# Two attention and expert layers on one core: a new order of steps from a finer event model, imposed on every engine, with a shared variance for two norms

## The chip, the core and the metric

The kernel runs on one core of a Trainium2 chip. A core has TensorE (PE, matrix products into the PSUM banks), VectorE (DVE), ScalarE (ACT), GpSimd (POOL) and SyncE (SP, which here only issues transfers). The metric is the device time of one execution in microseconds, lower is better. Before the change three runs gave 536.8, 538.77 and 545.6; the median is 538.77.

## The reference, cut to what matters

`x` is 4 sequences of 512 tokens with 128 features. Two layers, each of the form x = x + s·g:

```python
x = L0_attn_x
xn = _layernorm(x, axis=-1)
s = _L0_attn_ref(xn, ...)           # causal window of 64, 16 heads of 8, 4 value heads
g = _silu(_L0_ffn_ref(xn, ...))     # 2 * (one of 8 experts, 128 -> 512 -> 128, gelu)
x = x + s * g
xn = _layernorm(x, axis=-1)
s = _L1_attn_ref(xn, ...)           # norm, windowed attention, projection, norm, gelu feed-forward
g = _silu(_L1_ffn_ref(xn, ...))     # one of 8 experts, 128 -> 512 -> 128, relu
x = x + s * g
return x
```

Layer 0's attention first takes the mean over all keys of the sigmoid of each masked score, makes a weight per query of it, and only then the softmax of the weighted scores, so each score tile is made twice (a first pass for the sums, a second for the softmax). Its output is multiplied by `w_o`, and `b_o` is added. Layer 1's attention starts with a second layer norm of the already normed `xn`: two norms stand behind each other, with an affine step after the second that is folded into other data.

## The kernel before, in words

Tokens are cut into 16 tiles of 128 (4 batches b with 4 tiles t). Attention goes by tile. The experts go by block: `route` (L316) sorts the tokens by expert into 23 blocks of 128 rows per layer. It makes the rank of each token, a matrix `tok_blk` (L377), the comparison `in_place` (L385), a matmul `tokens`, and from these the indices `which` (L403, the expert of each block, which the weight loads read), `tokens_at` and `put_at` (L413). `moe_load` (L421) then loads a block's weights through SP (two of 256 KB and a few small ones) and gathers its rows by an indirect transfer from POOL (`xb`, L435). `moe_x` transposes the rows (copy to `xbT`, L448), `moe_h` makes `hb` with gelu (L503) or ReLU (L506) on ACT, `moe_y` adds the bias on DVE (`yb`, L473) and puts the rows back by an indirect transfer (`yt`, L474). `gates` (L481) reads a batch back and makes its gate on ACT and DVE (L490, L491).

The work is written as 30 generator threads (list at L1235). A thread yields what it needs next; `run` (L204) takes the step with the earliest modelled ready time, and among equals the one with the lower rank from the table. `spent` (L191) books the modelled cost of a step: TensorE time, and durations on DVE (D), ACT (A) and POOL (G). This fixes TensorE's order, for `mm` and `turn` (L81, L87) stamp each matmul. The order on DVE, ACT and POOL was left to the framework's scheduler, apart from a few `high_priority` and `keep_in_program_order` marks, and `nc.any` copies out of PSUM went to DVE or ACT as that scheduler chose.

The parts that the change touches:

- The row constants `rowb` (L127), `colb`, `wo0_sb` and `v1c` (L141) come through ACT's queue, the inputs and other weights through SP's.
- `layernorm` (L254) takes statistics on DVE (`bn_stats` L259, `bn_aggr` L260), adds eps (L236), takes the power on POOL (`rsqrt`, L237), and scales on DVE (L272) or, for layer 0, on ACT after an offset (L265, L267). Layer 0's norms run once per batch at the start; `prepare0` transposes them (copy to `xnT`, L536).
- `scores_q` (L757) is the first pass of layer 0. Each tile fills two pairs of PSUM banks; per pair ACT makes `th` (tanh, L786) and DVE reduces `mx` from the bank and `sm` from `th` (both L788).
- `outs0` (L902) transposes the attention output, divides (L910, L911), copies the transpose to `attT` (L920), multiplies by `w_o`, and adds row `o0` on DVE into `s` (L928). `combine0` (L933) computes x = acc·s + x on POOL (L938, L939).
- `prepare1` (L945) norms the new x (`xr`), sends it to memory for the experts, and makes the expert logits (`lg`, L518). `project1` (L970) norms `xr` again (`xh`) and projects it.
- In layer 1 the maxima of the scores are at L1055, the copies `shd` at L1063, the exponentials at L1098 (layer 0: L880), the copies `osb` at L1121 (layer 0: L898), the context copy at L1173. `feed1` (L1176) adds the projection's bias to the residual on POOL (L1189), norms (`hn`), and does the feed-forward.

One fragment that a sentence can't say, the order of the first pass's readers (from L784):

```python
for gg in range(2):
    th = att_p.tile([P, 2, J * QW], F32, tag="th", name=f"th_{b}_{t}_{gg}", bufs=2)
    nc.scalar.activation(th, ps[gg], AF.Tanh, scale=0.5 * SCALE)
    for dst, src, op in ((mx, ps[gg], ALU.max), (sm, th, ALU.add)):
        nc.vector.tensor_reduce(
```

Of the kernel before, what the change touches and what calls it, by code (L numbers as in the profile page):

```python
# [9 lines left out]
F32 = mybir.dt.float32  # L10
# [47 lines left out]
def two_layers(  # L58
# [68 lines left out]
    nc.scalar.dma_start(rowb, rows.partition_broadcast(P))  # L127
    colb = weight(cols, [P, NCOL], "colb", engine=nc.scalar)
    wo0_sb = weight(wo0, [P, D], "wo0_sb", engine=nc.scalar)
# [7 lines left out]
    for c in range(2):  # L137
        for a in range(2):
            r = slice(64 * c + 32 * a, 64 * c + 32 * a + 32)
            nc.sync.dma_start(wproj_sb[r], wproj_h[c, a])  # L140
            nc.scalar.dma_start(v1c[r], v1_h[c, a, :, :, None])  # L141
# [31 lines left out]
    now = {"T": 6.0, "S": 0.0, "-": 0.0}  # L173
    free = [0.0] * 4
    busy = {e: [] for e in "DAGQ"}
    at = {}

    def slot(e, t, n):
# [5 lines left out]
        while True:  # L184
            t = max(t, b[i - 1][1]) if i else t
            if i == len(b) or t + n <= b[i][0]:
                b.insert(i, (t, t + n))
                return t + n
            i += 1

    def spent(cost, steps=(), events=(), scores=0):  # L191
        now["T"] += 1.12 * cost
        t = max(now["T"], now["-"]) + 0.2
        for i, (e, n) in enumerate(steps):
            t = slot(e, t, n) + 0.1 if e else t + n
            if i + 1 == scores:
                now["S"] = max(now["S"], t)
            if cost and not scores and i == 0:

                free.append(t)  # L200
        for e in events:
            at[e] = t

    def run(threads):  # L204

        asked = [(g, ranks, next(g)) for g, *ranks in threads]
        while asked:
# [22 lines left out]
            asked[i : i + 1] = [(g, ranks, new)] if new else []  # L230

# [22 lines left out]
    def layernorm(src, name, dst, scalar=False):  # L254

        mv = small.tile([P, NT, 2], F32, tag="mv", name=f"mv_{name}")
        for t in range(NT):
            st = small.tile([P, 6], F32, tag="st", name=f"st_{name}_{t}")
            nc.vector.bn_stats(st, src[:, t, :])  # L259
            nc.vector.bn_aggr(mv[:, t, :], st)  # L260
        rs = small.tile([P, NT], F32, tag="rs", name=f"rs_{name}")
        rsqrt(rs, mv[:, :, 1], LN_EPS)
        if scalar:
            off = small.tile([P, NT], F32, tag="off", name=f"off_{name}")
            nc.vector.scalar_tensor_tensor(off, mv[:, :, 0], -1.0, rs, ALU.mult, ALU.mult)  # L265
            for t in range(NT):
                nc.scalar.activation(  # L267
                    dst[:, t, :], src[:, t, :], AF.Identity, bias=off[:, t : t + 1], scale=rs[:, t : t + 1]
                )
            return  # L270
        for t in range(NT):
            nc.vector.tensor_scalar(  # L272
                dst[:, t, :], src[:, t, :], mv[:, t, 0:1], rs[:, t : t + 1], ALU.subtract, ALU.mult
            )

# [40 lines left out]
    def route(mask, n):  # L316
# [7 lines left out]
        with tc.high_priority():  # L324
# [53 lines left out]
            spent(0.35, [("D", 6.5)], [("rows", n)])  # L378
        yield "M", [("rows", n)]
        with tc.high_priority():  # L380
            ps = bank(f"tokens_{n}")
            for q in range(2):
                in_place = att_p.tile([P, NTOK // 2, P], BF16, tag="th", name=f"in_place_{n}_{q}", bufs=2)
                i = q * NTOK // 2
                nc.vector.tensor_tensor(  # L385
                    in_place, placef[:, i : i + NTOK // 2, None].to_broadcast([P, NTOK // 2, P]),
                    place_at[:, None, :].to_broadcast([P, NTOK // 2, P]), ALU.is_equal,
                )
                for u in range(NTOK // 2):
                    mm(  # L390
                        ps[:, 0 : 3 * NBLK], in_place[:, u, :], tok_blk[:, i + u].rearrange("p a k -> p (a k)"),
                        start=(i + u == 0), stop=(i + u == NTOK - 1),
                    )

            past = of([1, NBLK, E], "past")
            nc.vector.tensor_tensor(
                past, ends[0:1, None, :].to_broadcast([1, NBLK, E]),
                block_at[0:1, :, None].to_broadcast([1, NBLK, E]), ALU.is_le,
            )
            ofx = of([1, NBLK], "ofx")  # L400
            nc.vector.tensor_reduce(ofx, past, AX.X, ALU.add)
            which = of([1, NBLK], "which", I32)
            nc.vector.tensor_single_scalar(which, ofx, float(E - 1), ALU.min)  # L403
            tokf = of([P, NBLK], "tokf")
            nc.vector.tensor_copy(tokf, ps[:, NBLK : 2 * NBLK])
# [905 lines left out]
```

## Time and profile before

| | |
|---|---|
| median of three runs | 538.77 us |
| the profiled execution, its time | 559.01 us |
| its span (first to last instruction) | 557.3 us |
| mean granted TensorE clock | 0.874 |
| PE busy (5512 matmuls) | 416.5 us, 75% |
| DVE busy (992) | 346.3 us, 62% |
| ACT busy (496) | 257.9 us, 46% |
| POOL busy (255) | 189.9 us, 34% |
| moved by transfers | 42.08 MB, mean 76 GB/s |

The profiled execution is one run under the profiler and is longer than the median; a sum made from its rows is a sum against 559.01. Busy time is an average over stages. The stages here are: the start with norms, projections and routing (0 to 100 us), layer 0's attention beside its experts (100 to 244), the passage from layer 0 to layer 1 (244 to 362), layer 1's attention beside its experts (362 to 530), and the last batch's tail. A wait is shown as the engine that waits, its line, and the instruction whose end released it.

### The profile page before, as it was taken

How to read it: one execution, taken by the hardware profiler on the slowest of the kernel's cores; microseconds unless marked ns; L12 is line 12 of the kernel's file. 1: busy time of each engine (PE TensorE's matmuls, PEld its weight loads, DVE VectorE, ACT ScalarE, POOL GpSimd, SP SyncE). 2: the span in 40 equal slices, each digit the busy share in tenths (PEclk: the TensorE clock that was granted, in tenths of full speed). 3: DMA queues.
4: the chain of work that ended last, by engine and by line, in shares of the span. 5: the costliest groups of instructions: out<-in, count | busy, mean ns of one | idle time of the engine just before them, and what ended most of it. 6: DMA issues, size and time to landing. Idle time of an engine off the chain costs nothing. (4 is left out here: it accounts for less than half of the span.)

```text
span 557.3 us, 14273 instructions
## 1 busy us (share of the span) xinstructions
PE 416.5 (75%) x5512; PEld 295.9 (53%) x5512; DVE 346.3 (62%) x992; ACT 257.9 (46%) x496; POOL 189.9 (34%) x255
## 2 busy tenths in 40 slices
PE   1455347978886796876668595789997989978956
PEld 0343124656563475542435363577776867767654
DVE  4359858345675676677746679276736663747383
ACT  2312134577576445555233232257672665435721
POOL 4820033333442343027332320465634422333210
PEclk9957557898999988989669968799998999979998
DMA  5300612344333333002100001534563222340121
GB/s 161 95 11 1 171 44 58 84 131 117 89 108 103 102 89 95 8 16 76 38 21 2 1 21 43 149 98 133 142 170 102 51 61 42 85 110 22 54 75 39
DMA packets 61732, 42.08 MB, mean 76 GB/s; under 512 B 11297, under 2 KB 54049, under 8 KB 61665
## 3 DMA queue, kind: packets, MB, share of 16 engines
q1 hardware_dynamic: 58144, 34.47, 22.6%
q0 software_dynamic: 2944, 6.04, 4.4%
q8 instruction: 44, 0.72, 0.5%
q10 hardware_dynamic: 576, 0.66, 0.4%
q14 instruction: 24, 0.19, 0.1%
HBM read 34.99 MB, written 6.16 MB: 74 GB/s over the span
## 5 line engine op out<-in xcount | busy, mean ns | idle before, releaser
L474 POOL DMA_INDIRECT yt<-yb,put_at x46 | 46.7, 1016 | 114.2 <-DVE yb L473 56.8
L435 POOL DMA_INDIRECT xb<-xd,tokens_at x46 | 46.3, 1007 | 104.3 <-PE xt L88 50.4
L83 PE MATMUL y<-wb,hb 128*128 128x128 f32 x368 | 56.3, 308 | 3.6 <-issue 3.6
L83 PEld LDWEIGHTS y<-wb,hb 128*128 128x128 f32 x368 | 51.9, 220 | 9.3 <-issue 6.7
L83 PE MATMUL h<-xbT,wb 128*128 128x128 f32 x368 | 51.5, 288 | 2.5 <-DVE xbT L448 1.2
L83 PEld LDWEIGHTS h<-xbT,wb 128*128 128x128 f32 x368 | 46.9, 201 | 9.3 <-issue 6.0
L83 PE MATMUL e<-q,kd 32*64 32x256 f32 (+1 forms) x864 | 45.8, 471 | 6.2 <-DVE mx L1055 5.8
L1055 DVE TENSOR_REDUCE mx<-s 128x16 f32<-128x1024 f32 x32 | 37.7, 1219 | 17.5 <-PE s L83 13.2
L786 ACT ACTIVATE th<-s 128x768 f32<-128x768 f32 x32 | 24.3, 810 | 44.7 <-PE s L83 25.4
L1098 ACT ACTIVATE pt<-e 128x1024 f32<-128x1024 f32 x32 | 31.0, 1021 | 29.6 <-PE e L83 27.7
L788 DVE TENSOR_REDUCE mx<-s 128x8 f32<-128x768 f32 x32 | 30.4, 951 | 21.9 <-ACT th L786 21.9
L880 ACT ACTIVATE pt<-e 128x1024 f32<-128x1024 f32 x32 | 31.0, 1021 | 24.6 <-PE e L83 24.5
L83 PE MATMUL ov<-pt,va 64*32 64x128 f32 (+1 forms) x896 | 36.8, 310 | 3.1 <-issue 1.5
L83 PE MATMUL s<-k,qd 32*32 32x384 f32 (+1 forms) x1024 | 37.6, 473 | 0.5 <-ACT pt L1098 0.5
L506 ACT ACTIVATE hb<-h,bb 128x128 f32<-128x128 f32 x92 | 25.9, 375 | 17.0 <-PE h L83 12.1
L788 DVE TENSOR_REDUCE sm<-th 128x8 f32<-128x768 f32 x32 | 30.1, 942 | 0.0
L1014 POOL TENSOR_TENSOR q<-qd,jmask 128x640 f32<-128x640 f32 x16 | 20.0, 1256 | 27.8 <-PE e L83 16.1
L83 PEld LDWEIGHTS e<-q,kd 32*64 32x64 f32 x864 | 19.7, 145 | 18.1 <-issue 12.6
L1121 ACT COPY osb<-ov 128x512 f32<-128x512 f32 x19 | 10.8, 587 | 37.5 <-issue 24.6
L83 PEld LDWEIGHTS <-diag 32*32 32x32 bf16 (+1 forms) x304 | 5.5, 90 | 42.1 <-issue 40.6
L503 ACT ACTIVATE hb<-h,bb 128x128 f32<-128x128 f32 x92 | 25.7, 382 | 1.8 <-PE h L83 1.7
L83 PEld LDWEIGHTS ov<-pt,va 64*32 64x32 f32 (+1 forms) x896 | 19.5, 112 | 12.0 <-issue 4.0
(271 smaller groups left out, 905.4 us busy)
## 6 DMA issues: line engine op xcount, KB each, us to landing
wb<-in_w SPq DMA_DIRECT2D x92, 256.0 KB
bb<-in_b SPq DMA_DIRECT2D x46, 64.0 KB
acc<-yt SPq DMA_DIRECT2D x8, 256.0 KB
x<-in_x SPq DMA_DIRECT2D x4, 256.0 KB
xd<-ln_a SPq DMA_DIRECT2D x4, 256.0 KB
xd<-xr SPq DMA_DIRECT2D x4, 256.0 KB
out<-acc SPq DMA_DIRECT2D x8, 128.0 KB
bb<-in_cols SPq DMA_DIRECT2D x46, 2.0 KB
```

The lines of the kernel that those rows point to most:

```text
L83: ins = nc.tensor.matmul(*args, **kw)
L435: nc.gpsimd.indirect_dma_start(out=xb, out_offset=None, in_=xd, in_offset=bass.IndirectOffsetOnAxis(ap=tokens_at[:, k : k + 1], axis=0),)
L474: nc.gpsimd.indirect_dma_start(out=yt, out_offset=bass.IndirectOffsetOnAxis(ap=routed[n][0][:, k : k + 1], axis=0), in_=y, in_offset=None,)
L503: nc.scalar.activation(dst, src, AF.Gelu, bias=bias)
L506: nc.scalar.activation(dst, src, AF.Relu, bias=bias)
L786: nc.scalar.activation(th, ps[gg], AF.Tanh, scale=0.5 * SCALE)
L788: nc.vector.tensor_reduce(dst[:, t, 8 * gg : 8 * gg + 8].rearrange("p (u j) -> p u j", u=2), src.rearrange("p u (j f) -> p u j f", j=J), A ...
L880: nc.scalar.activation(pt[:, 2 * gg : 2 * gg + 2], ps[gg], AF.Exp)
L1014: engine.tensor_tensor(dst, src[:, None, o : o + TW].to_broadcast([P, J, TW]), jmask[:, :, None].to_broadcast([P, J, TW]), ALU.mult,)
L1055: nc.vector.tensor_reduce(mx.rearrange("p a g j -> p g a j")[:, 2 * gg : 2 * gg + 2], ps[gg], AX.X, ALU.max, negate=True,)
L1098: nc.scalar.activation(pt[:, 2 * gg : 2 * gg + 2], ps[gg], AF.Exp, scale=SCALE)
L1121: nc.any.tensor_copy(osb[:, :, :, w].rearrange("p a j f -> p (a j) f"), ov[w].rearrange("p a c d f -> p (a c d) f"))
```

## The change

- The event model knows more: slots for DVE, ACT and POOL in single steps, the ACT function tables ("Ae" for exp, "Ag" for gelu, 1.3 us for a switch), new durations, new ranks for the 30 threads. `traced` collects the instructions that each step issued, `spent` notes each one's modelled start, and `settle` links the instructions of DVE, ACT and POOL in the order of these starts. So the model's order holds on all engines.
- `copied` and `sooner` choose DVE or ACT for the copies out of PSUM by the model; so do layer 1's ReLU and the four masked copies k4 of layer 0. Copies to `shd` are always on ACT.
- `layernorm_twice`: the second norm of layer 1 takes no statistics. The normed data have mean 0 and variance v/(v+eps), so both scales come from v, by one power of eight columns; `xh` is made on ACT from x itself.
- Layer 0's sums: row `o0` is added by a matmul of one row per 128 tokens into the same bank; acc·s and + x are on DVE, straight from the bank where the gate is there in time, otherwise from a copy.
- `scores_q`: both maxima stand ahead of both tanh.
- `route`: no longer at high priority; `in_place` uses the buffers of layer 0's `osb` instead of those of `th`, `which` is made after it.
- Layer 0's norms: batches 0 to 2 at once, batch 3 after the first transpose. Only the first part of `rowb` stays on ACT's queue; the rest, `colb`, `wo0_sb` and `v1c` go to SP's.
- In `feed1` the residual's two bias additions on POOL are moved: one ahead into `contexts1`, one to just after the norm.

By the built program, TensorE gets 16 matmuls more, DVE has 11 k4 copies of 16 and 28 of the 92 ReLU pieces, ACT has 26 table loads where it had 32, and POOL loses 12 larger operations. TensorE's order is nearly the old one; in the tail, batch 2's last feed-forward steps now stand ahead of batch 3's projection.

```diff
         load_x(b)
     wqkv0_sb = weight(wqkv0, [P, 296], "wqkv0_sb")
     rowb = wts.tile([P, NROW], F32, tag="rowb", name="rowb")
-    nc.scalar.dma_start(rowb, rows.partition_broadcast(P))
-    colb = weight(cols, [P, NCOL], "colb", engine=nc.scalar)
-    wo0_sb = weight(wo0, [P, D], "wo0_sb", engine=nc.scalar)
+    first = _ROWS["o0"].start
+    nc.scalar.dma_start(rowb[:, 0:first], rows[0:first].partition_broadcast(P))
+    nc.sync.dma_start(rowb[:, first:NROW], rows[first:NROW].partition_broadcast(P))
+    colb = weight(cols, [P, NCOL], "colb")
+    wo0_sb = weight(wo0, [P, D], "wo0_sb")
...
     def spent(cost, steps=(), events=(), scores=0):
         now["T"] += 1.12 * cost
         t = max(now["T"], now["-"]) + 0.2
...
         for i, (e, n) in enumerate(steps):
-            t = slot(e, t, n) + 0.1 if e else t + n
+            if e and len(e) > 1:
+                t = max(t, now["table"])
+                if table[0] != e:
+                    n, table[0] = n + 1.3, e
+            if e:
+                t = slot(e[0], t, n)
...
+                    steps_of[e[0]] += [(t - n, len(steps_of[e[0]]) + k, x) for k, x in enumerate(ins[: share if same > 1 else None])]
+                if len(e) > 1:
+                    now["table"] = t
+                t += 0.1
+            else:
+                t += n
             if i + 1 == scores:
                 now["S"] = max(now["S"], t)
             if cost and not scores and i == 0:
 
                 free.append(t)
+        assert not runs, (steps, [(e, len(r)) for e, r in runs])
         for e in events:
             at[e] = t
...
             at[e] = t
 
+    def sooner(cost, a, d, start=0.0):
+
+        t = max(now["T"] + 1.12 * cost, now["-"], start) + 0.2
+        ends = {}
+        for e, n in (("A", a), ("D", d)):
+            ends[e] = slot(e, t, n, take=False)
+        return min(ends, key=ends.get)
+
+    def copied(dst, src, cost, events=(), a=0.6, d=0.7):
+        e = sooner(cost, a, d)
+        (nc.scalar.copy if e == "A" else nc.vector.tensor_copy)(dst, src)
+        spent(cost, [(e, a if e == "A" else d)], events)
+
+    def settle():
+
+        for e, steps in steps_of.items():
+            steps.sort(key=lambda s: s[:2])
+            for (*_, one), (*_, next_) in zip(steps, steps[1:]):
+                tc.add_manual_dep(
+                    next_, one.name, mybir.DependencyInfo(mybir.DependencyClass.NoSync, mybir.DependencyReason.DATA),
+                    reason="order",
+                )
+
     def run(threads):
 
+        traced(skip=True)
...
+        settle()
 
...
+    def layernorm_twice(src, b, dst):
+
+
+        mv = moments(src, f"b{b}")
+        w = small.tile([P, 2, NT], F32, tag="w2", name=f"w2_{b}", bufs=1)
+        nc.vector.tensor_scalar_add(w[:, 0], mv[:, :, 1], LN_EPS)
+        nc.vector.reciprocal(w[:, 1], w[:, 0])
+        nc.vector.tensor_tensor(w[:, 1], w[:, 1], mv[:, :, 1], ALU.mult)
+        nc.vector.tensor_scalar_add(w[:, 1], w[:, 1], LN_EPS)
+        rs = small.tile([P, 2, NT], F32, tag="rs2", name=f"rs2_{b}", bufs=1)
+        nc.gpsimd.tensor_tensor(
+            rs.rearrange("p a t -> p (a t)"), w.rearrange("p a t -> p (a t)"),
+            neghalf[:, 0:1].to_broadcast([P, 2 * NT]), ALU.pow,
+        )
+        for t in range(NT):
+            nc.vector.tensor_scalar(
+                dst[:, t, :], src[:, t, :], mv[:, t, 0:1], rs[:, 0, t : t + 1], ALU.subtract, ALU.mult
+            )
+        both = small.tile([P, 2, NT], F32, tag="twice", name=f"twice_{b}", bufs=B)
+        nc.vector.tensor_tensor(both[:, 1], rs[:, 0], rs[:, 1], ALU.mult)
+        nc.vector.scalar_tensor_tensor(both[:, 0], mv[:, :, 0], -1.0, both[:, 1], ALU.mult, ALU.mult)
+        return both[:, 0], both[:, 1]
 
...
-            spent(0.35, [("D", 6.5)], [("rows", n)])
-        yield "M", [("rows", n)]
-        with tc.high_priority():
-            ps = bank(f"tokens_{n}")
-            for q in range(2):
-                in_place = att_p.tile([P, NTOK // 2, P], BF16, tag="th", name=f"in_place_{n}_{q}", bufs=2)
...
+            spent(0.35, [("D", 1.0)] * 7, [("rows", n)])
+        in_places = []
+        for q in range(2):
+            in_place = att_p.tile([P, NTOK // 2, P], BF16, tag="osb0", name=f"in_place_{n}_{q}")
+            i = q * NTOK // 2
...
+                in_place, placef[:, i : i + NTOK // 2, None].to_broadcast([P, NTOK // 2, P]),
+                place_at[:, None, :].to_broadcast([P, NTOK // 2, P]), ALU.is_equal,
+            )
+            in_places.append(in_place)
...
+        which = of([1, NBLK], "which", I32)
+        nc.vector.tensor_single_scalar(which, ofx, float(E - 1), ALU.min)
+        spent(0, [after(("rows", n))] + [("D", 0.75)] * 4, [("places", n)])
+        yield "M", [("places", n)]
+        ps = bank(f"tokens_{n}")
+        for i in range(NTOK):
...
-            spent(0.13, [("A", 0.3)], [("mx", n, k)])
+            copied(x_k, ps[:, 0:P], 0.13, [("mx", n, k)], 0.28, 0.28)
 
...
+        return "Ag", 1.5
+
+    def relu(h, src, bias):
+        e = sooner(0.92, 1.5, 1.4)
+        for c in range(FC):
+            dst, src_c, b = h[:, c, :], src[:, c * P : (c + 1) * P], bias[:, c : c + 1]
+            if e == "A":
+                nc.scalar.activation(dst, src_c, AF.Relu, bias=b)
+            else:
+                nc.vector.tensor_scalar(dst, src_c, b, 0.0, ALU.add, ALU.max)
+        return e, 1.5 if e == "A" else 1.4
...
+    def norm0(b):
+        xns[b] = tok.tile([P, NT, D], F32, tag="ln", name=f"ln_a{b}", bufs=3)
         layernorm(x_sb[b], f"a{b}", xns[b], scalar=True)
         put_tokens(xd0, b, xns[b])
-        spent(0, [("D", 2.2), ("G", 1.0), ("D", 0.2), ("A", 1.5)], [("ln0", b)])
+        spent(0, [(None, 1.5 * b), ("D", 1.5), ("G", 1.0), ("D", 0.2), ("A", 1.7)], [("ln0", b)])
...
+    traced(skip=True)
+    with tc.high_priority():
+        for b in range(3):
+            norm0(b)
...
+            if b == 0:
+                norm0(3)
             yield "M", [("xnT0", b)]
...
                     )
+            def over_keys(dst, src, gg, op):
+                nc.vector.tensor_reduce(
+                    dst[:, t, 8 * gg : 8 * gg + 8].rearrange("p (u j) -> p u j", u=2),
+                    src.rearrange("p u (j f) -> p u j f", j=J), AX.X, op,
+                )
+
+            for gg in range(2):
+                over_keys(mx, ps[gg], gg, ALU.max)
+            spent(1.5, [("D", 1.9)], scores=1)
             for gg in range(2):
                 th = att_p.tile([P, 2, J * QW], F32, tag="th", name=f"th_{b}_{t}_{gg}", bufs=2)
                 nc.scalar.activation(th, ps[gg], AF.Tanh, scale=0.5 * SCALE)
-                for dst, src, op in ((mx, ps[gg], ALU.max), (sm, th, ALU.add)):
-                    nc.vector.tensor_reduce(
-                        dst[:, t, 8 * gg : 8 * gg + 8].rearrange("p (u j) -> p u j", u=2),
-                        src.rearrange("p u (j f) -> p u j f", j=J), AX.X, op,
-                    )
-            spent(1.3, [("D", 1.9)], scores=1)
-            spent(0, [("A", 1.65), ("D", 1.9)], [("s0", i)], scores=1)
+                over_keys(sm, th, gg, ALU.add)
+                spent(0, [("A", 0.83), ("D", 0.95)], [("s0", i)], scores=1)
 
     def fitness0():
 
         for b in range(B):
-            yield "M", [("s0", b * NT + NT - 1), ("ke", (b - 1) * NT - 1)]
+            yield "-", [("s0", b * NT + NT - 1)]
             mx, sm = mxs[b]
             qk = qks[b]
 
...
-            yield "M", [("attT", b), ("xnT0", B - 1)]
+            copied(attT, transposed(att0[b], f"att_{b}"), 0.5, [("attT", b)])
+            yield "M", [("attT", b)] + ([("x1", b - 1)] if b - 1 in s0 else [])
             ps = bank(f"s0_{b}")
             for u in range(NT):
-                mm(ps[:, u * D : (u + 1) * D], attT[:, u * P : (u + 1) * P], wo0_sb, start=True, stop=True)
-            s = tok.tile([P, NT, D], F32, tag="xt", name=f"s0_{b}", bufs=B)
-            s0[b] = s
-            nc.vector.tensor_tensor(
-                s, ps.rearrange("p (t d) -> p t d", t=NT), row("o0")[:, None, :].to_broadcast([P, NT, D]), ALU.add
-            )
-            spent(1.1, [("D", 0.7)], [("so", b)])
+                o = ps[:, u * D : (u + 1) * D]
+                mm(o, ones[0:1, :], row("o0")[0:1], start=True, stop=False)
+                mm(o, attT[:, u * P : (u + 1) * P], wo0_sb, start=False, stop=True)
+            ps = ps.rearrange("p (t d) -> p t d", t=NT)
+            if at.get(("gate", 0, b), 1e9) < now["T"] + 3.0:
+                combine(b, ps)
+                spent(1.5, [("D", 0.7), ("D", 0.7)], [("so", b), ("x1", b), ("acc", 0, b)])
+            else:
+                s0[b] = tok.tile([P, NT, D], F32, tag="s0", name=f"s0_{b}", bufs=1)
+                copied(s0[b], ps, 1.5, [("so", b)])
+
+    def combine(b, s):
+
+        acc = accs.pop((0, b))
+        nc.vector.tensor_tensor(acc, acc, s, ALU.mult)
+        nc.vector.tensor_tensor(x_sb[b], acc, x_sb[b], ALU.add)
 
...
             yield "-", [("x1", b)]
             xn = tok.tile([P, NT, D], F32, tag="xt", name=f"xr_{b}", bufs=B)
             xrs[b] = xn
-            layernorm(x_sb[b], f"b{b}", xn)
+            twice[b] = layernorm_twice(x_sb[b], b, xn)
             put_tokens(xd1, b, xn)
...
         for b in range(B):
             yield "-", [("xn1", b), ("s1", (b - 1) * NT - 1)]
-            xh = tok.tile([P, NT, D], F32, tag="ln", name=f"xh_{b}", bufs=B)
-            layernorm(xrs[b], f"c{b}", xh)
-            at["xh", b] = slot("D", slot("G", slot("D", at["xn1", b], 2.3), 1.0) + 0.2, 1.4)
+            xh = tok.tile([P, NT, D], F32, tag="ln", name=f"xh_{b}", bufs=3)
+            scaled(xh, x_sb[b], *twice[b])
+            spent(0, [("A", 1.7)], [("xh", b)])
...
-            nc.any.tensor_copy(shd, transposed16(shb.rearrange("p a g r -> p a (g r)"), 2, f"sh1_{b}_{t}"))
+            nc.scalar.copy(shd, transposed16(shb.rearrange("p a g r -> p a (g r)"), 2, f"sh1_{b}_{t}"))
             sh4 = att_p.tile([P, 2, J, P], BF16, tag="sh4_1", name=f"sh4_1_{b}_{t}")
             for j in range(J):
...
+                nc.gpsimd.tensor_tensor(xrs[b], xrs[b], projb[:, None, :].to_broadcast([P, NT, D]), ALU.add)
+                spent(0, [("G", 1.6)], [("res", b)])
...
-            nc.gpsimd.tensor_tensor(res, res, projb[:, None, :].to_broadcast([P, NT, D]), ALU.add)
             nc.vector.tensor_tensor(res, ps.rearrange("p (t d) -> p t d", t=NT), res, ALU.add)
-            hn = tok.tile([P, NT, D], F32, tag="ln", name=f"hn_{b}", bufs=B)
+            hn = tok.tile([P, NT, D], F32, tag="ln", name=f"hn_{b}", bufs=3)
             layernorm(res, f"d{b}", hn)
-            spent(1.9, [("D", 0.7), ("D", 2.3), ("G", 1.0), ("D", 1.4)], [("pr", b)])
...
+            nc.gpsimd.tensor_tensor(res, res, row("ffn2")[:, None, :].to_broadcast([P, NT, D]), ALU.add)
+            spent(0, [after(("pr", b)), ("G", 1.3)])
             yield "M", [("pr", b)]
             hT = tok.tile([P, T], F32, tag="hT", name=f"hT_{b}", bufs=1)
```

## The prediction

> **What bounds the kernel now.** I read the share of busy time first (TensorE 75%, DVE 62%, ACT 46%, POOL 34%), cut the span into stages by what the work is, then read TensorE's waits, and then the timeline at each long one. The stages (columns: window, length, busy time of PE, its weight loads, DVE, ACT, POOL, then granted clock, DMA share, GB/s):
>
> ```profile
> 0.00:100.00 100.00, 47.62 (x367) 31.31 (x368) 63.40 (x210) 28.94 (x52) 34.25 (x94) 0.70 0.27 75
> 100.00:244.00 144.00, 116.67 (x1422) 79.73 (x1420) 89.38 (x198) 87.32 (x160) 46.75 (x51) 0.94 0.34 90
> 244.00:362.00 118.00, 82.89 (x1176) 52.49 (x1183) 77.34 (x245) 37.83 (x60) 39.85 (x38) 0.81 0.16 43
> 362.00:530.00 168.00, 152.32 (x2473) 119.94 (x2458) 100.67 (x297) 97.56 (x217) 66.37 (x71) 0.97 0.34 89
> 530.00:557.30 27.30, 17.03 (x96) 12.39 (x94) 15.51 (x43) 6.21 (x11) 2.68 (x2) 0.87 0.20 58
> ```
>
> TensorE idles 52.4, 27.3, 35.1, 15.7 and 10.3 us in these five, 140.8 in all. No engine is full in the first or third stage, so those are chains of dependent steps; in the fourth TensorE is busy 91%, so little can be taken there. Who ends TensorE's waits (total, times, longest):
>
> ```profile
> PE s L83 <- DVE mx L788: 22.6, 13, 7.9
> PE tr_xn L88 <- ACT ln_a L267: 12.4, 1, 12.4
> PE e L83 <- DVE mx L788: 8.7, 7, 2.4
> PE s L83 <- DVE attT L920: 7.6, 1, 7.6
> PE tokens L83 <- DVE in_place L385: 6.3, 2, 4.9
> PE e L83 <- DVE mx L1055: 6.1, 2, 5.8
> ...
> PE tr_o L88 <- DVE lg L518: 4.5, 1, 4.5
> PE tokens L83 <- DVE tok_blk L377: 4.3, 1, 4.3
> ```
>
> Two things stand out. Layer 0's score tiles wait for the maxima that DVE takes from their banks (L788), and the long single waits of the third stage are on DVE. The DVE timeline before TensorE's 7.6 us wait:
>
> ```profile
> 267.28 1.11 DVE L272 TENSOR_SCALAR xh<-xr,mv_c,rs_c 128x128 f32<-128x128 f32 x4 [0.71 <-POOL rs_c L237]
> 268.31 0.48 DVE L259 BATCH_NORM_STATS2 st_b<-x 128x6 f32<-128x128 f32 x2
> 268.71 0.16 DVE L260 BATCH_NORM_AGGREGATE mv_b<-st_b 128x2 f32<-128x6 f32 x1
> 268.79 0.66 DVE L920 COPY attT<-tr_att 128x512 f32<-128x512 f32 x1
> ```
>
> One 0.66 us copy that TensorE needs stands behind the chained norm (xh) of another batch and even behind statistics that nothing needs yet: a wrong order, not a shortage of DVE.
>
> **What the Trainium skill says.** "PSUM — Partial Sum Buffer", section "PSUM bank collisions raise a hardware error": two engines may not be in one bank and quadrant at once, two readers included. So th (ACT) and mx (DVE) of one bank must take turns; the trace agrees, DVE mx waits 21.9 us in 14 places for ACT th. "ScalarE: Activation LUTs", section "What ACT_TABLE_LOAD costs": 1283 ns for the load, 2.66 us with the drain; the trace shows 32 loads of 1283 ns, and the drain is no row in it. "TensorE: Matmul & The Clock Gate", Part 1: idling drops the clock to half and sustained activity restores it; here eight h matmuls take 0.89 us at full clock and 2.08 at half, and about 141 us of the execution are at half clock. The same page, under "Architectural detail", calls ACT's and DVE's queues strictly first in, first out; the copy above agrees.
>
> **The change part by part.** Sums are on the profiled execution (559.01 us, of which 557.3 are the span and 1.7 lie around it). The median of the three runs, 538.77, is 0.9638 of it; I scale by that at the end.
>
> *mx before th (L786, L788).* Before, a tile reads th0, mx0, sm0, (th1 beside sm0), mx1, sm1. With th 0.81, mx 0.95, sm 0.94, the second bank comes free 0.81+0.95+0.94+0.95 = 3.65 us after its scores. After, mx0, mx1, th1: 0.95+0.95+0.81 = 2.71, so 0.94 earlier. The second stage holds 14.2 us of these waits in 14 places (s 9.3, e 4.9); 14 × 0.94 = 13.2 is the most. Some will be ended by another thing, such as ACT's own queue: I take −10 (−4 to −16; a table load less there is in the lower end).
>
> *The order pinned on DVE, ACT and POOL.* By itself it does no work. It pays where a late DVE step holds TensorE: in the third stage attT 7.6, mx of layer 1 6.1, lg 4.5, tok_blk 4.3, osb of layer 1 3.4, together 25.9. Not all can vanish, for batch 3's x must be finished, normed and routed before the experts of layer 1 can start. The next two edits shorten that chain. I take −18 (−8 to −24) for all three.
>
> *Chained norm from the first variance.* Per batch it removes 4 st_c (0.275), 4 aggregates (0.171) and a pow from the chain, and adds about seven small DVE operations at the 0.17 of the L236 row: 1.8 against 1.2 us. The scaling, 4 × 0.44, goes from DVE to ACT (4 × 0.48 by the L267 row). From x to xh I count 10.5 us before and 7.5 after. DVE loses 16 × 0.446 + 16 × 0.441 − 4.8 = 9.4 us, ACT gains 7.7; ACT has 80 us free in that stage. Counted in the −18. If ACT were full there, it would cost its 1.9 us per batch.
>
> *Layer 0 sums from the bank.* Removed: four 0.69 us adds on DVE (L928) and 1.28 + 1.38 on POOL per batch (L938, L939). Added: two DVE operations of about 0.69 (row L491: 0.68) and 16 one-row matmuls. No row shows a one-row matmul; the nearest are 128-column ones at 0.11 (full clock) and 0.29 (mean of h). 16 × 0.11 to 16 × 0.29 is 1.8 to 4.6, and none hidden, since TensorE waits beside attT anyway: I take +2. The combine itself is 1.3 shorter per batch, also in the −18.
>
> *Fewer table loads.* The built program has 26 in place of 32, and in the part that matches the fourth stage 5 in place of 11. The loads there before:
>
> ```profile
> L503 ACT ACT_TABLE_LOAD x16 | 20.5, 1283 | 0.3
> L1098 ACT ACT_TABLE_LOAD x5 | 6.4, 1283 | 4.6 <-PE e L83 4.5
> ```
>
> 6 × 1.28 = 7.7 us of ACT (16 with the skill's drain). TensorE has only 15.7 us idle there; I take −4 (−8 to +6: a fixed order may put a late step ahead of a ready one in the densest stage).
>
> *Copies and ReLU by the model.* 7 blocks' ReLU go to DVE, all shd copies and 5 k4 masks to ACT: about 10 us each way. Nothing, while DVE is at 60% and ACT at 58% of the fourth stage; without that cover it is 1.5 us per block.
>
> *Start: layer norm 0, DMA queues, routing.* I walked the new order with the old durations. DVE now waits for POOL's pow before xnT_0 (POOL has masks to build), so xnT_0 comes at 19 instead of 15.7; q and k are normed at 37.6 instead of 42.1; the expert mask at 47.4 instead of 43.5; the last routing row (put_at) at 69.3 either way. Moving colb, wo0 and v1c from ACT's queue to SP's, past the inputs and the rest of rowb, frees ACT's first norm of a wait for v1c (8.9 to 9.9), but the norm's off is late as well. 0 (−4 to +4).
>
> *Tail.* After batch 3's last context, the new TensorE order puts batch 2's last feed-forward steps before batch 3's projection. TensorE idles 10.3 there, so most is hidden: +1 (0 to +4).
>
> Sum: −10 −18 +2 −4 +0 +0 +1 = −29. 559.01 − 29 = 530.0, × 0.9638 = 511.
>
> **The rivals.**
> (A) The stalls only move. DVE's work and TensorE's order are nearly the same, and each named wait may be followed by the next step of the same chain. Then the third stage gives nothing: −10 −4 +2 +1 = −11, 548 × 0.9638 = 528. For it: POOL's pow and the routing chain remain. Against it: the rows above show unneeded work ahead of needed work.
> (B) More than forecast, since shorter idling keeps the clock up. All 25.9 gone, 14.2 of mx, 7.7 of table loads, and the third stage's clock from 0.81 to 0.94: 82.9 × (1 − 0.81/0.94) = 11.5. Less 3 added: −56, 503 × 0.9638 = 485. Against it: it needs each to come in full.
> (C) Slower. ACT's order is now fixed by a model. In the 16 layer 0 score tiles th can stand behind a gelu of an expert block or an exp whose own input is late; then both banks stay taken, and TensorE's next scores wait. To be over 2% slower (549.5, that is 570.2 profiled, +11.2) it has to eat the other 29 as well: 40.2 / 16 = 2.5 us per tile. ACT's th waited 14.1 us in 4 places for the h of an expert block before, up to 4.8 each, so 2.5 is possible in a tile, but in all 16 it needs a model that is wrong everywhere.
> (D) It does not do what it says: the fixed order equals the old in the stalls. The result is A's.
>
> **How the numbers follow.** Forecast 0.55 (its own range 497 to 525), A with D 0.20, B 0.14, C 0.11. About 2% is what a measurement of this kernel can tell from no change: 528 to 549.5. A straddles that edge: 0.09 faster, 0.11 the same; of C 0.03 is the same and 0.08 slower. Faster 0.55 + 0.14 + 0.09 = 0.78, same 0.14, slower 0.08. The range 484 to 537 takes in A with the bad ends of the start and the tail (+8 profiled) and B's figure; it leaves out about half of B and most of C.
>
> **What would show it.** Right: the waits of s and e for mx fall from 31.3 to under 15; those on attT, lg, tok_blk and layer 1's mx are gone or under 2 each; the third stage is 15 us or more shorter, and xh follows x by 7 to 8 us; 26 table loads; put_at still near 69. Wrong: ACT's th waiting behind hb or pt, a third stage of the same length with new names in TensorE's waits, a start that is over 4 us longer, or a fourth stage with TensorE under 88%.

## The result and the profile after

The changed kernel takes 542.71 us (median of 20 runs, 540.39 to 547.49), the kernel before 538.77 (20 runs, 532.79 to 547.9): a ratio of 1.0118, with an interval of 1.0086 to 1.0149. It is a little slower, where 511 and a range of 484 to 537 were forecast. The ratio compares fast executions alone, those up to 1.5% above the fastest of their kernel (all 20 after, 13 of 20 before), so it lies above the quotient of the two medians.

The stages of the profile after, cut at the same events as below (end of the first put_at, of the second, of the last put; columns: window, length, busy time of PE, its weight loads, DVE, ACT, POOL, then granted clock, DMA share, GB/s):

```profile
0.00:68.50 68.50, 27.46 (x164) 18.44 (x165) 42.79 (x169) 17.16 (x32) 22.63 (x80) 0.89 0.29 82
68.50:332.40 263.90, 221.49 (x2851) 143.21 (x2851) 180.29 (x447) 151.94 (x276) 81.49 (x88) 0.86 0.24 66
332.40:507.50 175.10, 150.40 (x2418) 121.08 (x2420) 108.21 (x300) 82.85 (x190) 71.92 (x74) 0.92 0.37 96
507.50:541.20 33.70, 22.63 (x131) 15.11 (x117) 17.04 (x45) 10.34 (x15) 2.53 (x3) 0.81 0.22 65
```

Against the first profile of before (put_at at 69.3 and 350.3, last put at 524.9) the middle is 17 us shorter and layer 1's attention with its experts the same. But that profiled execution, with its 559.0 us, is above all 20 plain runs of its kernel. A second profile of the kernel before (first experiment) is the fairer measure; there layer 1 takes 159.5 us, and after it takes 175.1. TensorE's waits after the change:

```profile
PE s L83 <- ACT th L925: 19.9, 14, 8.6
PE xt L88 <- DMA xb<-xd,tokens_at: 16.7, 8, 3.7
PE e L83 <- POOL q L977: 6.5, 3, 3.9
...
PE s L83 <- DVE attT L263: 1.1, 2, 0.8
...
PE e L83 <- DVE mx L1194: 1.0, 2, 0.5
```

The long waits on attT, on layer 1's maxima, lg and tok_blk are gone, as forecast. The maxima of layer 0 no longer end a wait of the scores; the tanh that now stands behind them does. New is the second line: a block's transposition waits for its gathered rows, which are POOL's work. The masked q of the third line is POOL's work too, and not new: the scores waited 0.4 us for it in the first profile of before and 3.3 in the second. POOL's waits before, and then after the change:

```profile
POOL yt L474 <- DVE yb L473: 56.8, 15, 11.1
POOL xb L435 <- PE xt L88: 50.4, 15, 11.3
```

```profile
POOL yt L579 <- DVE yb L577: 84.7, 21, 12.2
...
POOL yt L579 <- DMA yt<-yb,put_at: 29.3, 10, 4.2
```

POOL stands 114 us in front of puts (68.7 before: 56.8 and 11.9), for the block's result on DVE or for the landing of the put before. Nothing is seen to pass a waiting put in either kernel: both profiles of before start POOL's 255 instructions in one and the same order, both of the changed kernel their 243. What differs is where the gathers stand in that order. When a gather is issued (from the fifth of a layer on), the gathers ahead of it are four to seven more than the puts in the kernel before, and one to three more in the changed one. The POOL timeline of one such place, and TensorE's line for the block whose gather it holds up:

```profile
404.96 1.05 POOL L311 TENSOR_TENSOR rs_d<-rs_d,neghalf 128x4 f32<-128x4 f32 x1 [8.42 <-DVE rs_d L310]
406.21 1.14 POOL L579 DMA_INDIRECT yt<-yb,put_at  x1 [0.20 <-issue]
...
412.68 0.99 POOL L579 DMA_INDIRECT yt<-yb,put_at  x1 [3.92 <-DMA yt<-yb,put_at]
417.35 0.97 POOL L579 DMA_INDIRECT yt<-yb,put_at  x1 [3.67 <-PE f L83]
...
419.76 1.01 POOL L541 DMA_INDIRECT xb<-xd,tokens_at  x1 [0.16 <-issue]
```

```profile
424.19 0.45 PE L88 MATMUL xt<-ident,xb 128*128 128x128 f32 x1 [3.69 <-DMA xb<-xd,tokens_at]
```

The three puts had their rows from DVE by 405.7, so the second waits for the landing of the put before, as its line says, and the third most likely too (the profile names PE's f, which that put doesn't read). The gather at 419.76 is the first since 386.43. In the median, without the first four gathers of each layer, a gather before the change was issued 28 us (layer 0) and 21 us (layer 1) ahead of its transposition; after it, 4.4 and 8.4 us, and 19 of all 46 had under 5 us.

Why the gathers came to stand there can be read in `moe_load` (L529 of the changed kernel; the same in the old one). It books a block's weight loads and its gather as one step, which may start when y of the block four earlier is done, since the weights take over that block's buffers. The put of that earlier block is booked from the same moment on, so the order made from the bookings sets the gather behind it. The gather itself needs only the buffer `xb`, which is free once the earlier block is transposed: it was issued 0.7 and 1.5 us after that before the change (medians of the two layers), and 17 and 21 us after it in the changed kernel. A version that books the gather by `xb` alone was not run.

### The profile page after: what moved, and what is told of

Read it like the earlier page. It is cut to its first block, busy times and chain, and to the rows that moved or that the text cites. A ratio compares the mean times of both kernels' runs of the same rounds, so it can differ in the third digit from the quotient of the medians.

```text
span 541.2 us, 14293 instructions
## 1 busy us (share of the span) xinstructions
PE 422.0 (78%) x5544; PEld 297.8 (55%) x5544; DVE 348.3 (64%) x959; ACT 262.3 (48%) x512; POOL 178.6 (33%) x243
## 4 chain that ended last, share of the span: by engine, by line
PE 44%; DVE 21%; ACT 9%; DMA 9%; issue 8%; POOL 8%; SPq 0%; POOLq 0%; ACTq 0%; DVEq 0%
PE s L83 9%; PE e L83 7%; PE y L83 5%; PE h L83 5%; DMA xb<-xd,tokens_at 4%; DMA yt<-yb,put_at 4%; PE ov L83 3%; PE fy L83 3%; ACT th L925 3%; PE f L83 2%; DVE mx L915 2%; ACT pt L1014 2%; DVE mx L1194 2%; PE o L88 1%; DVE xr L372 1%
## 5 line engine op out<-in xcount | busy, mean ns | idle before, releaser
L83 PE MATMUL e<-q,kd 32*64 32x256 f32 (+1 forms) x864 | 47.3, 479 | 7.4 <-POOL q L977 6.5
L83 PE MATMUL y<-wb,hb 128*128 128x128 f32 x368 | 52.8, 295 | 0.1
L83 PEld LDWEIGHTS y<-wb,hb 128*128 128x128 f32 x368 | 48.7, 208 | 5.6 <-ACT hb L608 2.5
L925 ACT ACTIVATE th<-s 128x768 f32<-128x768 f32 x32 | 26.0, 812 | 45.7 <-DVE mx L915 44.9
L1014 ACT ACTIVATE pt<-e 128x1024 f32<-128x1024 f32 x32 | 31.0, 1021 | 20.3 <-PE e L83 20.2
L83 PE MATMUL s<-k,qd 32*32 32x384 f32 (+1 forms) x1024 | 39.1, 510 | 0.9 <-DVE k L1155 0.5
L83 PE MATMUL ov<-pt,va 64*32 64x128 f32 (+1 forms) x896 | 31.3, 302 | 4.6 <-DVE att L1290 4.4
L263 ACT COPY osb<-ov 128x512 f32<-128x512 f32 x36 | 20.1, 589 | 29.4 <-PE ov L83 26.1
L608 ACT ACTIVATE hb<-h,bb 128x128 f32<-128x128 f32 x92 | 25.9, 379 | 2.4 <-PE h L83 2.3
L88 PE MATMUL xt<-ident,xb 128*128 128x128 f32 x46 | 14.0, 316 | 16.7 <-DMA xb<-xd,tokens_at 16.7
L616 ACT ACTIVATE hb<-h,bb 128x128 f32<-128x128 f32 x64 | 18.2, 374 | 15.6 <-PE h L83 12.3
L83 PEld LDWEIGHTS ov<-pt,va 64*32 64x32 f32 (+1 forms) x896 | 18.1, 111 | 11.4 <-issue 5.9
```

Of the source, the lines that this page charges most:

```text
L83: ins = nc.tensor.matmul(*args, **kw)
L88: ins = nc.tensor.transpose(dst, src, ident)
L263: (nc.scalar.copy if e == "A" else nc.vector.tensor_copy)(dst, src)
L608: nc.scalar.activation(h[:, c, :], src[:, c * P : (c + 1) * P], AF.Gelu, bias=bias[:, c : c + 1])
L1014: nc.scalar.activation(pt[:, 2 * gg : 2 * gg + 2], ps[gg], AF.Exp)
```

## The experiments

Ratios are to runs of the kernel before on the same chip, with 95% intervals; a difference of two ratios is turned into time with 538.8 us.

**Both kernels profiled again**, without an edit.

> The kernel before, unchanged, profiled a second time. Theory 1: the first profiled execution (span 557.3) was some 20 us longer than usual, and the excess lies in single late DVE and ACT steps of the third stage, the same that the prediction priced as gain; then this span is 533 to 541, the second put_at ends by 330 to 338 in place of 350.3, and the waits on attT, lg, tok_blk and osb together are under 15 us in place of 19.8. Rival: the excess was spread over all stages (a lower clock); then each stage is 3 to 4% shorter and those waits are still near 20.

Measured: span 531.8, second put_at 340.2. TensorE's waits there:

```profile
PE s L83 <- DVE attT L920: 7.6, 1, 7.6
...
PE e L83 <- DVE mx L1055: 6.1, 2, 5.8
PE tokens L83 <- DVE tok_blk L377: 5.0, 1, 5.0
...
PE tr_o L88 <- DVE lg L518: 4.0, 1, 4.0
```

So theory 1 fell: the priced waits are nearly the same in a shorter execution (only the 3.4 us on osb is gone). The rival isn't met as written either: start and tail are as long as in the first profile, and the excess lies in the middle (11.0 us) and in layer 1's stage (15.1). The clock records of the first profile add up to 141.3 us at half clock, here 91.0. Half of that difference is 25.2, and the spans differ by 25.5, but only 13.5 of these are longer busy time of TensorE (416.5 against 403.0). That the clock made the whole excess is not shown. The stages:

```profile
0.00:70.20 70.20, 28.84 (x184) 19.51 (x200) 44.12 (x177) 15.65 (x29) 22.64 (x82) 0.89 0.32 87
70.20:340.20 270.00, 204.53 (x2727) 132.97 (x2703) 185.14 (x468) 135.04 (x235) 92.45 (x95) 0.89 0.25 66
340.20:499.70 159.50, 148.75 (x2463) 119.04 (x2448) 103.87 (x301) 96.70 (x217) 72.24 (x76) 0.99 0.37 100
499.70:531.80 32.10, 20.91 (x171) 14.83 (x169) 17.03 (x47) 10.87 (x16) 2.69 (x3) 0.89 0.23 68
```

> The changed kernel, unchanged, profiled a second time. Its first profile (span 541.2) agrees with its median (542.7), so both theories expect a span of 538 to 544, the second put_at at 330 to 335, and TensorE's waits of xt for the gathered rows (16.7 us in 8 places) at 12 to 20 us.

Measured: 546.2 us, span 544.5, waits of xt on the gather 15.3 us in 6 places. The second put_at came at 339.0, later than expected, and the span is just above the band; 158.7 us were at half clock (131.3 in the first profile).

**POOL's order left free.**

```diff
     def settle():
         for e, steps in steps_of.items():
+            if e == "G":
+                continue
             steps.sort(key=lambda s: s[:2])
```

> The changed kernel with the order of POOL left to the framework's scheduler (DVE and ACT stay fixed). Theory 2: fixing POOL's order put the gathers of expert rows behind puts that wait for DVE and for the landing of the put before, so a gather now leads its transposition by about 4 us and not by 20; freed, the waits of xt on the gather fall from 16.7 to under 5, and the time falls by 8 to 15 us to 528 to 535. Rival: the gather is late because the block itself is late (its rows are asked for when the buffer comes free); then the waits only change their name and the time stays within 3 us of 542.7.

Measured: 515.91, ratio 0.967 (0.964 to 0.970): 24 us less than the change as it was, more than the 8 to 15 expected. Waits of TensorE and of POOL:

```profile
PE s L83 <- ACT th L927: 20.2, 14, 8.7
...
PE e L83 <- POOL q L979: 3.8, 1, 3.8
...
PE xt L88 <- DMA xb<-xd,tokens_at: 0.3, 1, 0.3
```

```profile
POOL yt L581 <- DVE yb L579: 36.4, 12, 6.3
...
POOL xb L543 <- PE xt L88: 32.3, 9, 7.6
```

A gather again waits for its buffer to come free (xb on xt), and leads by 18 and 24 us; the wait of xt is gone. The puts still wait 28.5 us for the landing of the put before (29.3 in the changed kernel), but the gathers stand further ahead of them, by four to seven again. The rival fell.

```profile
0.00:68.70 68.70, 27.80 (x164) 18.50 (x165) 42.72 (x169) 17.16 (x32) 22.61 (x82) 0.90 0.31 81
68.70:327.50 258.80, 221.05 (x2851) 144.11 (x2851) 179.88 (x448) 151.85 (x276) 86.82 (x90) 0.86 0.24 67
327.50:482.80 155.30, 142.53 (x2420) 114.60 (x2420) 107.15 (x300) 82.86 (x190) 66.87 (x70) 0.98 0.42 109
482.80:515.70 32.90, 21.80 (x128) 14.76 (x111) 17.04 (x45) 10.34 (x15) 2.52 (x2) 0.89 0.22 66
```

TensorE's work is the same as in the changed kernel; layer 1's stage is 20 us shorter. Of these, 12 us are idle time of TensorE that is gone (24.7 to 12.8), and 8 are shorter busy time, at a granted clock of 0.98 in place of 0.92.

**Which of POOL's steps.** Three kernels take different instructions out of the fixed order (`loose` holds the gathers, the puts, or both).

```diff
         for e, steps in steps_of.items():
+            steps[:] = [s for s in steps if s[2].name not in loose]
             steps.sort(key=lambda s: s[:2])
...
+            gather = nc.gpsimd.indirect_dma_start(
...
+            loose.add(gather.ins.name)
```

> The changed kernel with the order fixed on DVE, ACT and POOL as it is, except that the 46 gathers of expert rows are left out of POOL's fixed order. Theory 2 (the gathers stand behind puts that wait): the same 515 to 519 as with POOL's order free, a gather again leads its transposition by about 20 us, and the waits of xt on it are under 5 us. Rival: another POOL step (the masked q, the norms' powers, vx) was the late one, and gathers are only where it shows; then the time stays above 530.

Measured: 522.76, ratio 0.980 (0.971 to 0.989). Most of the loss is won back, but the time is above the 515 to 519 expected. The gathers lead by 18 and 23 us and no wait of xt on them is left.

> The changed kernel, with only the puts left out of POOL's fixed order; gathers and the other steps keep theirs. Theory 2 in the form 'puts hold up the gathers': without the puts in the line the gathers lead by 12 us or more again, 514 to 524. Rival: the gathers are held up by the norms' powers and the masked q ahead of them in the fixed order, not by puts; then the lead stays under 9 us and the time above 530.

Measured: 520.02, ratio 0.965 (0.960 to 0.971), a lead of 16 and 18 us: all of the loss is won back.

For the third only these two kinds keep a fixed order:

```diff
+            if e == "G":
+                steps[:] = [s for s in steps if s[2].name in loose]
```

> The changed kernel, with POOL's fixed order holding only among the gathers and puts of the experts; all other POOL steps are free, DVE and ACT fixed. Theory 2 (gathers behind puts that wait): nearly all of the loss stays, a gather leads its transposition by under 9 us, and the time is 530 to 545. Rival: about a third or more of the loss is of the other POOL steps; then 518 to 529.

Measured: 527.40, ratio 0.981 (0.974 to 0.988), with a lead as short as in the changed kernel (4.4 and 7.6 us) and 14.0 us of waits of xt. The rival's band holds it. So the fixed places of the puts are the cause, for without them nothing is lost. But the gathers behind them are not all: puts with gathers cost 0.014 (0.007 either way), puts with the other steps (gathers free) 0.013 (0.010 either way), puts with everything 0.045. In the third kernel the gathers come as late as in the changed one, and most of the time is won back all the same. Two late kinds of input together cost more than their sum; why that is so isn't shown.

**The maxima first, in the kernel before.**

```diff
+            for gg in range(2):
+                over_keys(mx, ps[gg], gg, ALU.max)
             for gg in range(2):
                 th = att_p.tile(...)
                 nc.scalar.activation(th, ps[gg], AF.Tanh, scale=0.5 * SCALE)
-                for dst, src, op in ((mx, ps[gg], ALU.max), (sm, th, ALU.add)):
-                    nc.vector.tensor_reduce(...)
+                over_keys(sm, th, gg, ALU.add)
```

> The kernel before with one part of the change alone: both maxima of a score tile ahead of both tanh. The prediction: 10 us less (4 to 16), so 523 to 535. Rival: DVE now frees the banks sooner, but th waits for mx and the sums are late by as much; TensorE's waits then end with ACT th, and the time stays within 3 us of 538.8.

Measured: 526.88, ratio 0.986 (0.981 to 0.991): 7.5 us less (2.6 either way), inside the 4 to 16. TensorE's waits of s and e on the pair of readers fell from 28.4 (second profile of before) to 19.8 us, and end with th:

```profile
PE s L83 <- ACT th L794: 14.6, 9, 5.7
...
PE e L83 <- ACT th L794: 5.2, 7, 2.1
```

The rival was right on the name of the wait, not on the time. This profile is of an execution of 532.8 us, above its kernel's median, so its waits may be on the long side.

**No engine's order fixed.**

```diff
             asked[i : i + 1] = [(g, ranks, new)] if new else []
-        settle()
```

> The changed kernel with no engine's order fixed: the framework's scheduler orders DVE, ACT and POOL as it did before, everything else of the change stays. If the fixed order of DVE and ACT is worth the prediction's share (most of its 18 us), this is 10 us or more slower than the 515.9 with POOL alone free: 526 to 536. Rival: the fixed order of DVE and ACT is worth nothing, and the gain comes from the other edits; then 513 to 519.

Measured: 518.24, ratio 0.968 (0.958 to 0.977), the same as with POOL alone free. So the order fixed on DVE and ACT, for which the event model was refined, is worth nothing in sum (0.001, 0.010 either way). The profiles show two parts that cancel: the first put_at ends at 60.5 in place of 68.7, and the rest takes 459 us in place of 447. The second part is less sure, for this profile has the lower clock (0.878 against 0.900), and which of the two made the 12 us isn't shown.

**The second norm from its own statistics**, booked at the old time, so that TensorE's order stays.

```diff
-            twice[b] = layernorm_twice(x_sb[b], b, xn)
+            layernorm(x_sb[b], f"b{b}", xn)
...
-            scaled(xh, x_sb[b], *twice[b])
+            layernorm(xrs[b], f"c{b}", xh)
```

> POOL's order free, and the second norm of layer 1 made from its own statistics again, on DVE, with TensorE's order kept. The prediction counted 3 us per batch of a shorter chain, inside the 18 of the third stage. If that chain bounds the third stage, this is 3 to 8 us slower: 519 to 524. Rival: batch 3's attention in layer 0 bounds that stage and the norm is hidden beside it for batches 0 to 2: 514 to 518.

Measured: 526.57, ratio 0.985 (0.977 to 0.993): 10 us slower, above both bands. TensorE waits 12.0 us for xh in 3 places, up to 6.1. TensorE's order was planned for the early xh, which may be part of it, so the 10 us (5 either way) are rather an upper bound of what the part is worth.

**The sums of layer 0 as before, and half of that.**

```diff
-                mm(o, ones[0:1, :], row("o0")[0:1], start=True, stop=False)
-                mm(o, attT[:, u * P : (u + 1) * P], wo0_sb, start=False, stop=True)
+                mm(ps[:, u * D : (u + 1) * D], attT[:, u * P : (u + 1) * P], wo0_sb, start=True, stop=True)
...
+            nc.vector.tensor_tensor(
+                s, ps.rearrange("p (t d) -> p t d", t=NT), row("o0")[:, None, :].to_broadcast([P, NT, D]), ALU.add
+            )
...
-        nc.vector.tensor_tensor(acc, acc, s, ALU.mult)
-        nc.vector.tensor_tensor(x_sb[b], acc, x_sb[b], ALU.add)
+        nc.gpsimd.tensor_tensor(acc, acc, s, ALU.mult)
+        nc.gpsimd.tensor_tensor(x_sb[b], acc, x_sb[b], ALU.add)
```

> POOL's order free, and layer 0's sums as before the change: no one-row matmuls, row o0 added on DVE, acc times s and + x on POOL; TensorE's other order kept. The prediction counted +2 us for the one-row matmuls and about 1.3 us per batch less for the combine. The profile shows the one-row matmuls at 0.42 us, 32 of them, 10.5 us of TensorE. If these stand in front of the sums on TensorE, undoing the part costs nothing or gains: 510 to 516. If the combine on DVE is worth what the prediction said, this is 2 to 5 us slower: 518 to 521.

Measured: 511.86, ratio 0.951 (0.945 to 0.956).

> POOL's order free, row o0 added on DVE as before, but the combine on DVE as in the change; TensorE's other order kept. Against 515.9: if the one-row matmuls lie on the path with their 10.5 us, up to 8 us less (508 to 513); if they run while TensorE would wait anyway, the same or up to 3 us more (515 to 519).

This one leaves the last four lines of the diff away. Measured: 512.92, ratio 0.949 (0.942 to 0.956). So the combine on DVE or POOL makes no difference that shows, and the one-row matmuls cost 0.017, or 9 us (about 3 either way). Their row, and that of the matmuls which they go with, in the profile with POOL's order free:

```profile
L83 PE MATMUL s<-wo_sb,attT 128*128 128x128 f32 x32 | 10.6, 425 | 0.4 <-DVE attT L263 0.4
L83 PE MATMUL s<-rowb,ones 1*128 1x128 f32 x32 | 10.5, 420 | 0.0
```

A record over one row takes as long as one over 128 (420 and 425 ns), and each of the 16 matmuls shows as two records, as the other float32 matmuls do: the 5512 matmuls of the table of before are records. Both means are over both clocks: a one-row record takes 321 ns at full clock and 497 at half.

**Versions that follow.** First, tanh takes one pair of banks while the maximum takes the other.

```diff
+            over_keys(mx, ps[0], 0, ALU.max)
+            nc.scalar.activation(ths[1], ps[1], AF.Tanh, scale=0.5 * SCALE)
+            over_keys(mx, ps[1], 1, ALU.max)
+            nc.scalar.activation(ths[0], ps[0], AF.Tanh, scale=0.5 * SCALE)
```

> POOL's order free, and in each score tile of layer 0 ACT's tanh takes the second pair of banks while DVE's maximum takes the first, and then the other way round (same TensorE order). TensorE's waits s on th (20.2 us in 14 places, up to 8.7) say that the second pair comes free 2.71 us after its scores; swapped, it is 1.9. Theory: up to 14 x 0.8 = 11 us, some of it hidden: 506 to 512. Rival: ACT reaches th late for other work, so the order within the tile gives nothing: 514 to 518.

Measured: 511.33, ratio 0.955 (0.949 to 0.961), 6 us less than without it (4 either way). TensorE's scores wait for th in 7 places in place of 14, but nearly as long in all (20.2 us without the swap):

```profile
PE s L83 <- ACT th L929: 18.5, 7, 9.4
```

So the gain is measured, and the 0.8 us per tile as its cause is not shown.

Then DVE and ACT keep the model's order only from the first routing on:

```diff
+            steps[:] = [s for s in steps if s[0] >= at["routed", 0]]
             steps.sort(key=lambda s: s[:2])
```

> POOL's order free, the tanh of the two bank pairs swapped, and the order of DVE and ACT fixed only from the first routing on. With nothing fixed the first put_at ended at 60.5 in place of 68.7, and with DVE and ACT fixed the rest took 447 in place of 459. If the two parts add, 8 us less than the 511 of the swap alone: 500 to 505. Rival: the earlier start only waits at the next place, or the fixed order of DVE and ACT was worth nothing and the two spans differed by the clock: 508 to 512.

Measured: 506.96, ratio 0.942 (0.936 to 0.947), and the first put_at ends at 60.6 (68.8 with the swap alone). That is 7 us less (4 either way), close to the 8 of the earlier start, between the band and the rival's. Its profiled execution (505.7) is no faster than that of the swap alone (504.9, where its median is 511.3), so the profiles don't show that the earlier start is kept to the end.

> The same as the one with the fixed order from the first routing on, and with row o0 added on DVE in place of the one-row matmuls. Whatever that part gives with POOL's order free it should give here too: 494 to 502 if the one-row matmuls are on the path, 500 to 506 if not.

Measured: 501.28, ratio 0.928 (0.922 to 0.935): the fastest here, 7% under the kernel before. The time lies in both bands; the 0.014 (0.009 either way) that the ratio fell by agree with the 9 us of these matmuls found above.

## Why the prediction was wrong

The step that failed is "the order pinned on DVE, ACT and POOL. By itself it does no work. It pays where a late DVE step holds TensorE". I priced what a fixed order gives on DVE, and its harm on ACT alone (rival C). For POOL I took nothing and named no instruction that waits, though the change fixes its order as well, and though the page of before had the rows that matter: yt idle 56.8 us for DVE's yb, and xb idle most for its own buffer, since the old order had it well ahead of the puts. Shown by the runs: POOL's fixed order costs 0.045, or 24 us, all of it through the places of the puts. Without it the kernel is at 0.967, or 521 us on the scale of 538.8: inside the range, and 10 above 511. The Trainium skill, in the section that I cited for ACT and DVE ("TensorE: Matmul & The Clock Gate", "Architectural detail"), says the same of GpSimd: "GPSIMD is per-Q7 strict FIFO", that is, first in, first out on each of GpSimd's cores. The traces agree, with POOL's 243 instructions in the same order in both profiles of the changed kernel.

Step by step, with POOL's order free and the second profile of before beside it:

- *mx before th*, −10: the right mechanism; alone in the kernel before it gave −7.5 (2.6 either way). What remained is the wait for th behind mx.
- *Third stage*, −18: the middle went from 270.0 to 258.8, that is −11.2. Of it −7.5 is mx and +9 the one-row matmuls, so about −13 is left for this term, an estimate from two profiles at different clocks (0.89 and 0.86). The four waits went as forecast; the chain from x to xh did not get 3 us shorter (batch 0: 9.3 us before, 13.9 after), against the 7 to 8 named as a sign of being right. The order itself gave at most part of it: with no order fixed the middle takes 263.2, and the whole the same time. That the chained norm gave most of the 13 is likely from its run (about 10), not shown apart.
- *One-row matmuls*, +2: 9 ± 3. I took 16 records of 0.11 us; the 16 matmuls are 32 records that keep TensorE busy for 10.5 us in all, a count that the two records of every such matmul in the page (368 for 46 blocks of 4) could have told. The 0.11 is about the distance of records of h from start to start; eight of them take 1.06 us at full clock, not the 0.89 that I gave.
- *Table loads*, −4: 26 as forecast, and layer 1's stage fell from 159.5 to 155.3 with POOL free. No run has the table loads apart, so that the 4.2 agree may be luck. In the changed kernel it is 175.1, with TensorE busy 86%, the sign that I had named for "wrong" (under 88%).
- *Start*, 0: the first put_at ends at 68.5, as worked out. What I didn't see is that without a fixed order it would end at 60.5.
- *Tail*, +1: 32.1 to 32.9 with POOL free, in one profile of each.

Added to 511, the misses are 24 (POOL), 7 (one-row matmuls), 2.5 (mx) and 5 (third stage), 549.5 in all, against 542.7 measured. Several of these terms are sure to 3 us or worse, so the sum shows POOL's as the largest and no more than that. Of the rivals, C had the right kind of cause, a step fixed behind one that waits, on the wrong engine. A and D fell, since the named waits did go. B did not come: the changed kernel had 131 and 159 us at half clock in its two profiles, the kernel before 141 and 91.

## What to carry to other kernels

When an order is fixed on an engine, go through that engine's long waits in the old profile, and ask for each what the new order sets behind it. Here the model booked the gather together with loads that could start only later, and the gather took over their place. A gather issued from a computing engine is work with a deadline far ahead: book it by what it needs itself (not tried here), and keep it out of a line with puts that wait for results. And take a second profile where the first lies outside the plain runs, before its microseconds are priced.

## What the runs showed of the hardware

- A record of a one-row float32 matmul of 128 columns took 420 ns, one of 128 rows 425 ns in the same place (mean over both clocks; two records each matmul).
- In both profiles of a kernel POOL started its instructions in the same order (255 before, 243 after), also where it stood idle for one of them.
- Two executions of one kernel differed by 25.5 us of span, with 141.3 and 91.0 us at half clock and nearly the same priced waits.
- In 20 runs of the changed kernel, though, the time did not follow the mean clock (0.859 to 0.890, correlation −0.07).
